# A fixed instruction order for the head of a decoder layer, layer norms on GpSimd, and two transposes moved to DMA

## The chip, the cores and the metric

The kernel runs on one core of one Trainium2 chip. The metric is the device time of one execution in microseconds (us), as the median of several runs. A hardware profiler gives a trace of one further execution; its span runs from the first to the last instruction. The engines are TensorE (PE, with its weight loads apart), VectorE (DVE), ScalarE (ACT), GpSimd (POOL) and SyncE (SP), which here only issues DMAs.

## What is computed

One decoder layer with pre-norms, on x of 8 sequences, 128 tokens, width 512, in float32. `ctx` has the same shape.

```python
x = x + attention(layernorm(x), w_q, w_k, w_v, w_o)   # 32 heads, 8 kv heads, head 128, causal
x = x + cross(ctx, ctx, layernorm(x))                 # softmax(ctx . q^T / sqrt(128)), one head
x = x + ffn(layernorm(x))                             # 4-bit weights, groups of 128 rows
# ffn: (silu(x Wg) * (x Wu)) Wd, inner width 1376
# W[k, n] = q[k, n] * s[g, n] - (z[g, n] + 1) * s[g, n],  g = k // 128
```

The layer norms have no weights; eps is 1e-5. The attention's weights are float32 and random; w_q is 512 x 4096, w_k and w_v 512 x 1024, w_o 4096 x 512.

## The kernel before, in words

**Number format.** PE works in float16 pairs. A tile is split into a high half (cast, on ACT) and a low half (value minus high half, on VectorE or GpSimd): `split` (L115). A product takes three matmuls, high x high, high x low, low x high: `mm3` (L131, L136 to L138). Weights are first brought to a common size: `sumsq` (ACT, L234) sums squares, `scales` casts the sums (L253), adds them over partitions by a matmul with ones (L257, L260) and makes a power-of-two-like factor from them on VectorE (L265, L273, L279). `convert` then scales and splits a weight, in one of two ways: `direct` on ACT and VectorE (L305, L306), or on GpSimd with a cast on ACT (L311, L116, L119).

**Work.** There are 8 kv groups g of 4 heads, and two halves of 4 sequences. A unit is one g and one half; a step is one sequence b of a unit, 64 steps in all. For a unit: `proj_k` (k for all 4 sequences, 12 matmuls of 512 columns), four `proj_q`, and every second group `proj_v` for a pair of groups. For a step: `att_s` (scores into `ps_sc`, masked minimum on VectorE L475, exps on ACT L433, a scaling of the reciprocal `rec` on GpSimd L443, multiplication on GpSimd L489, split into `pb`, and a DMA transpose of `pb` to `pt`, L503), `att_v` (probabilities times v, `ps_at`, L512, L513), and `att_o` (output projection into `ps_o`, added to the residual `xr` on VectorE, L529). v is copied by two DMAs into a second tile `vd` (L420) for the first 64 rows.

**Order.** The program goes through a scheduler that places every instruction by a simulated timeline, by its place in the source and its dependencies. `issue_after` (L122) adds an ordering edge without a wait where the source wants one. Each engine runs its own list in order; SP's list holds all DMAs, and a DMA that waits holds those behind it.

**Head.** The source of the head (after `load_x`, L654) loads x and weights in the order x0, wk, x1, wq in two pieces, x2, x3, wv, x4 to x7, wo, wq and wk of group 1. `load_h` computes a layer norm: statistics on VectorE (L144, L145, L147), the power -0.5 on GpSimd (L151), the application on VectorE (L152), four PE transposes (L347), and a split out of PSUM into the tiles `hTh` and `hTl` of that half. k and q of the first head are projected in three pieces, the first as soon as sequence 0 is there. Twelve warm-up matmuls on zeros (L696) stand in the source after that; the scheduler put them ahead of the first projection. Then come the other q, v, the scores of step 0, the sums of wo, the layer norms of sequences 4 to 7 and the four pieces of wo.

**Scales of the feed-forward weights.** In steps 3 to 5 `col_scales` (L548) loads rows of scales in pieces of 512 columns (L558), casts them to float32 (VectorE, L560), transposes them on PE by pieces of 128 columns (L563) into `ps_st`, copies them out (ACT, L567, L570), and derives ratios from them on VectorE (L573 to L581). In steps 3 to 6 `zeros` unpacks the zero points (VectorE, L602).

Of the kernel before, what the change touches and what calls it, by code (L numbers as in the profile page):

```python
# [18 lines left out]
P = 128  # L19
HQ = 64  # L20
B = 8
# [33 lines left out]
def tile_decoder(  # L55
# [75 lines left out]

    def mm3(ps, parts, start=True, stop=True):

        n = len(parts)
        for i, (lh, ll, rh, rl) in enumerate(parts):
            nc.tensor.matmul(ps, lh, rh, start=start and i == 0, stop=False)  # L136
            nc.tensor.matmul(ps, lh, rl, start=False, stop=False)  # L137
            nc.tensor.matmul(ps, ll, rh, start=False, stop=stop and i == n - 1)  # L138
# [22 lines left out]
    def bank(tag, shape, name):  # L161
# [15 lines left out]
    hT = [  # L177
        [hp.tile([P, KT, TH], F16, name=f"hT{p}{h}", tag=f"hT{p}{h}") for h in range(2)]
        for p in "hl"
    ]  # L180
# [63 lines left out]
    def scales(kind, g, cols=None):  # L244

# [12 lines left out]
        else:  # L258
            for i in range(m):
                nc.tensor.matmul(  # L260
                    ps[:, :1], ones, sb[:, i : i + 1], start=i == 0, stop=i == m - 1
                )
        norm = ONORM if kind == "o" else WNORM
# [15 lines left out]
        nc.vector.reciprocal(sc[:, c0:c1] if kind == "q" else sc, r)  # L279

    def soft_scale(g):
        t = small.tile([P, GH], F32, name="soft", tag="soft")
        nc.vector.tensor_scalar(
            t, sc_t["q", g], sc_t["k", g], -(ASCALE**2) / SCALE, ALU.mult, ALU.mult
        )
        nc.vector.reciprocal(t, t)
        two = small.tile([P, GH // 2], F32, name="soft2", tag="soft2")
        for i in range(2):
            rows = slice(i * HQ, (i + 1) * HQ)
            nc.vector.tensor_copy(  # L290
                two[rows], t[rows].rearrange("p (a i) -> p a i", i=2)[:, :, i]
            )
        soft_t[g] = two
# [38 lines left out]
    def prep_wv(pr, i):  # L332
# [3 lines left out]
        convert(hi, lo, raw_t["v", pr][:, 2 * i : 2 * i + 2, :], sc_t["v", pr])  # L336

    def prep_wo(g, j):
# [3 lines left out]
        convert(hi, lo, raw_t["o", g][:, j, :], sc_t["o", g])  # L342
# [7 lines left out]
    def load_h(b, tag="s"):  # L350
        half, bb = divmod(b, HB)
        h1 = work.tile([P, H], F32, name="h1", tag=tag, bufs=3 if tag == "s" else 1)
        ln = layernorm(h1, xr[b], ASCALE)
        ps = transpose4(h1, "o")
        cs = slice(bb * P, (bb + 1) * P)
        return ln + split(hT[0][half][:, :, cs], hT[1][half][:, :, cs], ps)
# [11 lines left out]
    def proj_q(g, half, j, pieces=(slice(0, TH),)):  # L368
# [7 lines left out]
        for cs in pieces:  # L376
            proj(ps[:, cs], wq_t[g * GH + j], half, cs)
            bs = slice(cs.start // P, cs.stop // P)
# [7 lines left out]
    def proj_k(g, half, pieces=((0, HB),)):  # L386
# [3 lines left out]
        for b0, b1 in pieces:  # L390
            cs = slice(b0 * P, b1 * P)
            proj(ps[:, b0:b1, :].rearrange("p b t -> p (b t)"), wk_t[g], half, cs)
            split(k2[:, b0:b1, 0, :], k2[:, b0:b1, 1, :], ps[:, b0:b1, :])
            yield

    def proj_v(pr, b):
# [14 lines left out]
        mm3(ps, parts)  # L411
        v = vp.tile([P, 2, 2 * P], F16, name="v", tag="v")
# [8 lines left out]
        v_t[pr, b] = v, vd  # L421

# [124 lines left out]

    def col_scales(m, after):  # L548
# [4 lines left out]
        nc.gpsimd.memset(sT[m], 1.0)  # L553
        ps = bank("j", [P, nt, ngr], "ps_st")
        for c0 in range(0, n, H):
            cw = min(n - c0, H)
            s16 = deqp.tile([P, 2 * H], F16, name="s16", tag="qr", bufs=2)
            nc.sync.dma_start(s16[:ngr, :cw], src[:, c0 : c0 + cw])  # L558
            s32 = deqp.tile([P, H], F32, name="s32", tag="qr", bufs=2)
            issue_after(nc.vector.tensor_copy(s32[:ngr, :cw], s16[:ngr, :cw]), after)  # L560
            for k in range(0, cw, P):
                w = min(P, cw - k)
                nc.tensor.transpose(  # L563
                    ps[:w, (c0 + k) // P, :], s32[:ngr, k : k + w], ident[:ngr, :ngr]
                )
        full = n // P
        nc.scalar.copy(sT[m][:, :full, :], ps[:, :full, :])  # L567
        if full < nt:
            w = n - full * P
            nc.scalar.copy(sT[m][:w, full, :], ps[:w, full, :])  # L570
# [16 lines left out]
    NZ = 2 * KT + NFT  # L587
    zt = {}
# [67 lines left out]
    load_x(0)  # L656
    fetch_wk(0)
    load_x(1)
    fetch_wq(0, ((0, 1), (1, GH)))
    load_x(2)  # L660
    load_x(3)
    fetch_wv(0)
    for b in range(HB, B):
        load_x(b)
    fetch_wo(0)
    fetch_wq(1)
    fetch_wk(1)
    halves = (slice(0, P), slice(P, 2 * P), slice(2 * P, 4 * P))
    kgen = proj_k(0, 0, ((0, 1), (1, 2), (2, 4)))
    qgen = proj_q(0, 0, 0, halves)  # L670
    ln0 = load_h(0, "s")
    sumsq("k", 0, 0, 0)
    scales("k", 0)
    ln1 = load_h(1, "s")
    sumsq("q", 0, 0, 0)
    scales("q", 0, (0, 1))
    prep_wk(0, True)
    next(kgen)
    ln2 = load_h(2, "s")
    ln3 = load_h(3, "h1")  # L680
    issue_after(ln1[0], ln0[2])
    issue_after(ln2[0], ln1[2])
    issue_after(ln2[2], ln1[4])
    issue_after(ln3[2], ln1[4])
    prep_wq(0, 0, True)
    next(qgen)
    next(kgen)
    next(qgen)
    next(kgen)
    next(qgen)  # L690

    warm = const.tile([P, TH], BF16, name="warm")
    nc.vector.memset(warm, 0.0)
    ps = bank("a", [P, TH], "ps_w")
    for _ in range(12):
        nc.tensor.matmul(ps, warm[:, :P], warm, start=True, stop=True)  # L696
# [420 lines left out]
```

## Time and profile before

| | |
|---|---|
| Runs | 697.48, 699.82, 700.36 us; median 699.82 |
| Profiled execution | 697.42 us, span 695.6 us |
| PE busy | 654.2 us (94%) |
| DVE busy | 493.3 us (71%) |
| ACT busy | 452.0 us (65%) |
| POOL busy | 375.6 us (54%) |
| Mean granted PE clock | 0.987 |

"Busy" is the time in which an engine runs an instruction. A row of a timeline gives start, length, engine, line of the kernel, operation, output and input by the program's names, their shapes, and in brackets how long the engine was idle before and what ended that. Two matmul rows overlap, since the matmuls are pipelined: the distance of their starts is what one costs. Where the profile speaks of L136 to L138 these are the three matmuls of `mm3`, whoever calls it.

### The profile page before, as it was taken

The numbers are of one execution on the slowest core, as the hardware profiler recorded it, in microseconds if no ns is written. First come the engines' busy times: TensorE is split into PE (matmuls) and PEld (weight loads), VectorE is DVE, ScalarE is ACT, GpSimd is POOL, SyncE is SP. The second block draws the span as 40 slices with busy tenths as digits, with TensorE's granted clock in tenths as the row PEclk, the third lists the DMA queues.
The fourth block names the chain that finished last, engine by engine and source line by source line (L and its number), as shares of the span: only waits on it lengthen the run. The fifth ranks groups of instructions, "written<-read, shape, count | busy, mean of one in ns | idle before, by whom it ended". The sixth has DMA issues, their size and how long they took to land.

```text
span 695.6 us, 12510 instructions
## 1 busy us (share of the span) xinstructions
PE 654.2 (94%) x4099; PEld 376.2 (54%) x4099; DVE 493.3 (71%) x1437; ACT 452.0 (65%) x1274; POOL 375.6 (54%) x573
## 2 busy tenths in 40 slices
PE   5689979999999999999999999999988799999995
PEld 3365544555555545555555555565555445565474
DVE  6774486766757786575778766666678789888986
ACT  4784373766567676655769665454575489968884
POOL 2885184955566896556589696645434723310110
PEclk9999989999999999999999999999999999999998
DMA  9555014455344476244444523422211100002002
GB/s 305 196 133 125 16 37 149 117 147 82 118 104 127 139 154 164 66 122 103 128 141 99 133 65 73 99 57 62 51 42 39 42 1 1 0 1 60 1 1 61
DMA packets 88367, 61.92 MB, mean 89 GB/s; under 512 B 54255, under 2 KB 71706, under 8 KB 88301
## 3 DMA queue, kind: packets, MB, share of 16 engines
q1 hardware_dynamic: 88300, 61.12, 34.1%
q8 instruction: 32, 0.52, 0.3%
q14 instruction: 35, 0.28, 0.1%
HBM read 42.12 MB, written 2.20 MB: 64 GB/s over the span
## 4 chain that ended last, share of the span: by engine, by line
PE 75%; ACT 7%; DVE 6%; POOL 5%; issue 4%; DMA 3%; SPq 0%; DVEq 0%; POOLq 0%; ACTq 0%
PE ps_q L136 7%; PE ps_q L137 7%; PE ps_q L138 7%; PE ps_c L941 7%; PE ps_o L136 7%; PE ps_o L138 7%; PE ps_o L137 7%; PE ps_c L942 6%; PE ps_v L138 2%; PE ps_v L137 2%; PE ps_v L136 2%; PE ps_k L136 2%; PE ps_k L137 2%; PE ps_k L138 2%; DMA pt<-pb 1%
## 5 line engine op out<-in xcount | busy, mean ns | idle before, releaser
L433 ACT ACTIVATE s<-s,negm 128x64 f32<-128x64 f32 (+1 forms) x256 | 93.3, 366 | 56.8 <-DVE negm L475 56.4
L136 PE MATMUL ps_q<-hTh,wqh 128*128 128x512 f16 (+2 forms) x264 | 99.5, 378 | 4.5 <-DVE rs L147 2.4
L137 PE MATMUL ps_q<-hTl,wqh 128*128 128x512 f16 (+2 forms) x264 | 99.3, 377 | 0.0
L138 PE MATMUL ps_q<-hTh,wql 128*128 128x512 f16 (+2 forms) x264 | 99.0, 376 | 0.0
L136 PE MATMUL ps_o<-woh,ah 128*128 128x512 f16 x256 | 98.1, 383 | 0.9 <-ACT ah L116 0.9
L137 PE MATMUL ps_o<-wol,ah 128*128 128x512 f16 x256 | 97.8, 382 | 0.0
L138 PE MATMUL ps_o<-woh,al 128*128 128x512 f16 x256 | 97.6, 381 | 0.0
L529 DVE SCALAR_TENSOR_TENSOR xr<-ps_o,unsc,xr 128x512 f32<-128x512 f32 x64 | 47.9, 749 | 56.6 <-PE ps_o L138 53.7
L443 POOL TENSOR_SCALAR rec<-rec 128x4 f32<-128x4 f32 x64 | 14.1, 221 | 125.7 <-DVE rec L441 125.2
L119 POOL TENSOR_TENSOR pb<-s,pb 128x128 f16<-128x128 f32 (+1 forms) x128 | 72.2, 578 | 7.8 <-ACT pb L116 6.0
L475 DVE CUSTOM_DVE_ANT_0 s<-ps_sc,mask,soft 128x64 f32<-128x64 f32 (+1 forms) x256 | 67.1, 311 | 9.7 <-PE ps_sc L138 7.5
L941 PE MATMUL ps_c<-h3h,nf 128*128 128x512 f16 (+1 forms) x176 | 65.9, 380 | 1.9 <-DVE ps_c L952 1.1
L489 POOL TENSOR_TENSOR s<-s,rec 128x128 f32<-128x128 f32 (+1 forms) x128 | 63.5, 517 | 4.7
L942 PE MATMUL ps_c<-h3l,nf 128*128 128x512 f16 (+1 forms) x176 | 65.7, 379 | 0.0
L119 DVE TENSOR_TENSOR ql<-ps_q,qh 128x512 f16<-128x512 f32 (+2 forms) x66 | 44.2, 669 | 29.4 <-ACT qh L116 29.1
L119 POOL TENSOR_TENSOR il<-pr,ih 128x512 fp32r<-128x512 f32 (+1 forms) x16 | 20.8, 1301 | 77.0 <-ACT ih L116 77.0
L116 ACT CAST ah<-ps_at 128x512 f16<-128x512 f32 x64 | 37.3, 583 | 34.4 <-PE ps_at L138 22.1
L116 ACT CAST pb<-s 128x128 f16<-128x128 f32 (+1 forms) x128 | 43.0, 350 | 25.3 <-POOL s L489 23.9
L116 ACT CAST qh<-ps_q 128x512 f16<-128x512 f32 (+2 forms) x66 | 37.2, 563 | 28.3 <-PE ps_q L138 26.4
L952 DVE TENSOR_SCALAR ps_c<-ps_c,rTg 128x512 f32<-128x512 f32 (+1 forms) x64 | 46.0, 751 | 5.8 <-PE ps_c L942 5.6
L119 DVE TENSOR_TENSOR al<-ps_at,ah 128x512 f16<-128x512 f32 x64 | 43.8, 685 | 6.3 <-ACT ah L116 6.1
L433 ACT ACTIVATION_READ_ACCUMULATOR s<-s,negm 128x1 f32 x256 | 48.1, 188 | 0.0
(196 smaller groups left out, 1766.6 us busy)
## 6 DMA issues: line engine op xcount, KB each, us to landing
rawo<-in_L_attn_w_o_dram SPq DMA_DIRECT2D x8, 1024.0 KB
rawq<-in_L_attn_w_q_dram SPq DMA_DIRECT2D x7, 1024.0 KB, 5.5
zi<-zd SPq DMA_DIRECT2D x26, 256.0 KB, 3.4
vd<-v SPq DMA_DIRECT2D x64, 64.0 KB, 2.1
qr<-_L_ffn_down_qweight_dram SPq DMA_DIRECT2D x10, 256.0 KB, 3.3
xr<-in_x_dram SPq DMA_DIRECT2D x8, 256.0 KB, 7.2
rawk<-in_L_attn_w_k_dram SPq DMA_DIRECT2D x8, 256.0 KB, 3.1
rawv<-in_L_attn_w_v_dram SPq DMA_DIRECT2D x4, 512.0 KB
```

What stands on the lines that cost most here:

```text
L116: a = nc.scalar.copy(hi, src)
L119: b = (lo_eng or nc.vector).tensor_tensor(lo, src, hi, ALU.subtract)
L136: nc.tensor.matmul(ps, lh, rh, start=start and i == 0, stop=False)
L137: nc.tensor.matmul(ps, lh, rl, start=False, stop=False)
L138: nc.tensor.matmul(ps, ll, rh, start=False, stop=stop and i == n - 1)
L433: exp = nc.scalar.activation(v, v, AF.Exp, bias=negm[:, j : j + 1], scale=-1.0, accum_out=sums[:, j : j + 1],)
L475: nc.vector.tensor_tensor_reduce(view, flat(ps, cols[j]), masks[j // 2], soft_t[g][:, j % 2 : j % 2 + 1], BIG, ALU.add, ALU.min, negm,)
L489: mul = nc.gpsimd.tensor_tensor(v, v, rec[:, 2 * k : 2 * k + 2].unsqueeze(2).to_broadcast([P, 2, (k + 1) * HQ]), ALU.mult,)
L529: return nc.vector.scalar_tensor_tensor(xr[b], ps, unsc_t[g], xr[b], ALU.mult, ALU.add)
L941: nc.tensor.matmul(ps, lh, rh, start=r == 0, stop=False, skip_group_check=r > 0)
L942: nc.tensor.matmul(ps, lh, rl, start=False, stop=True, skip_group_check=r > 0)
L952: nc.vector.tensor_scalar(ps, ps, sc, None, ALU.mult)
```

## The change

- **A fixed order.** `in_order` ties every instruction recorded within it to the one recorded before it on the same engine. The whole head, up to the first four v and the first two pieces of wo, moves into a function `begin` that is recorded within it. Generators (`yield` after the matmuls and after the evacuation) let the source interleave the steps by hand. After `begin` the scheduler decides as before.
- **Front.** Ten warm-up matmuls come first. The loads go x0, wk, x1, x2, x3, wq in one piece, wv, x4 to x7, the rest as before. k is projected in two pieces of two sequences, q whole.
- **Layer norms of the head on GpSimd.** VectorE makes the statistics and minus the mean; GpSimd the power and the application (L397 of the new kernel). Sequences 0 to 3 are transposed on PE as before. Sequences 4 to 7 are cast on ACT, their low half is made on GpSimd, and one DMA transpose for each brings both halves to `hT2`, which is now one tile for each half of the sequences. The tile that later takes the layer norm for the feed-forward is joined likewise.
- **Weights.** wv and the first two pieces of wo are converted in the `direct` way.
- **Scales.** All feed-forward scales are loaded into one float16 tile of 32 rows and transposed by one DMA; `col_scales` copies its columns out of that on VectorE.
- **soft_scale** computes two 64-row pieces directly instead of a product and two copies.

```diff
+    @contextmanager
+    def in_order():
+        traced = nc.cur_bb.bb.instructions
+        known = {id(i) for i in traced}
+        yield
+        last = {}
+        for i in nc.cur_bb.bb.instructions:
+            if id(i) in known:
+                continue
+            prev = last.get(i.engine)
+            if prev is not None:
+                tc.add_manual_dep(
+                    i,
+                    prev.name,
+                    mybir.DependencyInfo(
+                        mybir.DependencyClass.NoSync, mybir.DependencyReason.DATA
+                    ),
+                    reason="in_order",
+                )
+            last[i.engine] = i
...
-    hT = [
-        [hp.tile([P, KT, TH], F16, name=f"hT{p}{h}", tag=f"hT{p}{h}") for h in range(2)]
-        for p in "hl"
-    ]
+    hT2 = [hp.tile([P, 2, KT, TH], F16, name=f"hT{h}", tag=f"hT{h}") for h in range(2)]
+    hT = [[t[:, p, :, :] for t in hT2] for p in range(2)]
...
+    def ln_stats(b):
...
+        nc.vector.bn_stats(st, xr[b])
+        nc.vector.bn_aggr(mv, st)
+        rs = small.tile([P, 2], F32, name="rs2", tag="rs2")
+        nc.vector.tensor_scalar(
+            rs[:, 0:1], mv[:, 1:2], EPS, ASCALE**-2, ALU.add, ALU.mult
+        )
+        nc.vector.tensor_scalar(rs[:, 1:2], mv[:, 0:1], -1.0, None, ALU.mult)
+        ln_t["rs", b] = rs
+
+    def ln_apply(b):
+        rs = ln_t.pop(("rs", b))
+        rstd = small.tile([P, 1], F32, name="rstd", tag="rstd")
+        nc.gpsimd.tensor_tensor(rstd, rs[:, 0:1], mhalf, ALU.pow)
+        h = deqp.tile([P, H], F32, name="h", tag=("qr", "zi")[b % 2], bufs=2)
+        nc.gpsimd.tensor_scalar(h, xr[b], rs[:, 1:2], rstd, ALU.add, ALU.mult)
+        ln_t["h", b] = h
...
+    def h_dma(b):
...
+        hb = work.tile([P, 2, H], F16, name="hb", tag="hb")
+        split(hb[:, 0, :], hb[:, 1, :], ln_t.pop(("h", b)), nc.gpsimd)
+        nc.sync.dma_start_transpose(
+            hT2[half].rearrange("p a k t -> p (a k) t")[:, :, cs],
+            hb.rearrange("p a t -> p (a t)"),
+        )
...
+    def scales_load():
+        rows = deqp.tile([SROWS, NFT * P], F16, name="srow", tag="srow")
+        nc.gpsimd.memset(rows, 0.0)
+        for m in "gud":
+            _, _, src, ngr, n = quant[m]
+            nc.sync.dma_start(rows[zrow[m] : zrow[m] + ngr, :n], src)
+        zt["s"] = deqp.tile([P, NFT, SROWS], F16, name="scol", tag="scol")
+        nc.sync.dma_start_transpose(zt["s"], rows)
...
-        for c0 in range(0, n, H):
...
+        ins = nc.vector.tensor_copy(sT[m], zt["s"][:, :nt, zrow[m] : zrow[m] + ngr])
+        issue_after(ins, after)
...
+        kgen = proj_k(0, 0, ((0, 2), (2, 4)))
+        h = {b: h_pe(b) for b in range(HB)}
+        ln_stats(0)
+        sumsq("k", 0, 0, 0)
+        ln_apply(0)
+        sk = scales_parts("k", 0)
+        next(sk)
+        ln_stats(1)
+        next(sk)
+        ln_apply(1)
+        next(h[0])
+        ln_stats(2)
+        ln_apply(2)
+        next(h[0])
+        prep_wk(0, True)
+        next(h[1])
+        ln_stats(3)
+        ln_apply(3)
+        next(h[1])
+        next(h[2])
+        sumsq("q", 0, 0, 0)
+        next(h[3])
+        next(kgen)
...
+        next(q[0])
+        next(q[1])
+        prep_wq(0, 2, True)
+        h_dma(4)
+        ln_stats(6)
+        ln_apply(6)
+        prep_wq(0, 3, True)
+        h_dma(5)
+        next(q[1])
+        next(q[2])
+        prep_wv(0, 0, True)
+        ln_stats(7)
+        ln_apply(7)
+        h_dma(6)
+        prep_wv(0, 1, True)
+        soft_scale(0)
+        h_dma(7)
+        next(q[2])
+        next(q[3])
+        for i in range(2):
+            sumsq("o", 0, i, 0, 2)
+        next(so)
+        next(q[3])
+        v = [proj_v(0, b) for b in range(HB)]
+        next(v[0])
+        next(v[1])
+        next(so)
+        out_scale(0)
+        next(v[0])
+        att_s(0, 0)
+        next(v[2])
...
+    with in_order():
+        begin()
```

## The prediction

> **What bounds the kernel now.** First the page's second part, the busy tenths in 40 slices of 17.4 us. TensorE (PE) is short of full in slices 0 to 2, 5 and 29 to 31 and in the last; in between it is the bound. The change works on slices 0 to 2 and 5.
>
> ```profile
> PE   5689979999999999999999999999988799999995
> ```
>
> Next the table by stage (PE, weight load, DVE, ACT and POOL busy, granted PE clock, DMA share, GB/s).
>
> ```profile
> 12.90:50.00 37.10, 27.63 (x251) 19.74 (x250) 30.61 (x109) 28.75 (x85) 28.12 (x35) 1.00 0.60 193
> 50.00:84.00 34.00, 33.40 (x204) 18.60 (x203) 13.84 (x37) 13.89 (x39) 11.73 (x18) 1.00 0.36 81
> 84.00:94.00 10.00, 7.88 (x74) 4.99 (x73) 8.32 (x38) 8.46 (x37) 7.21 (x13) 0.99 0.11 22
> 94.00:104.00 10.00, 8.49 (x40) 3.89 (x40) 8.40 (x19) 6.12 (x20) 9.80 (x15) 0.84 0.21 42
> 104.00:110.00 6.00, 6.00 (x24) 2.57 (x25) 5.97 (x13) 2.29 (x6) 5.38 (x6) 0.72 0.47 131
> 110.00:510.00 400.00, 399.03 (x2675) 224.69 (x2674) 265.83 (x882) 251.34 (x817) 257.14 (x392) 1.00 0.43 107
> ```
>
> From 110 to 510 us PE idles 1 us of 400, so whatever the change wins or loses by 110 arrives at the end unshortened. Up to 12.9 us no projection runs; from there to 50 PE idles 9.5 us, from 50 to 84 0.6. From 84 to 104 it idles 2.1 + 1.5 = 3.6 us, and in 94 to 110 its clock falls. PE's timeline there shows what for: a scale transpose that waited for VectorE, then projections at half pace.
>
> ```profile
> 93.41 0.38 PE L563 MATMUL ps_st<-ident,s 4*128 4x4 f32 x4 [0.87 <-DVE rec L441]
> 94.05 0.58 PE L136 MATMUL ps_q<-hTh,wqh 128*128 128x512 f16 x1 [0.26 <-DVE r L273]
> ...
> 95.28 0.63 PE L136 MATMUL ps_q<-hTh,wqh 128*128 128x512 f16 x1
> 95.70 0.63 PE L137 MATMUL ps_q<-hTl,wqh 128*128 128x512 f16 x1
> ...
> 97.54 0.38 PE L136 MATMUL ps_q<-hTh,wqh 128*128 128x512 f16 x1
> 97.75 0.38 PE L137 MATMUL ps_q<-hTl,wqh 128*128 128x512 f16 x1
> ```
>
> Start to start is 0.43 us until 97, 0.215 after; 104 to 107.5 repeats it. The transposes cost a share of PE, the wait, and the clock.
>
> **What the Trainium skill says.** "TensorE: Matmul & The Clock Gate", Part 1: the array falls to half rate after an idle window of about 3.4 us and needs a busy one to come back. The 0.43 against 0.215 agrees. Part 4 there says transposes don't count as work for this gate; no row shows that alone. "SBUF — State Buffer", section "SBUF: two separate sides": VectorE and GpSimd hold a common port pair exclusively, for a whole instruction. The trace agrees: two 64x2 copies took 2.04 us while GpSimd multiplied weights.
>
> ```profile
> 22.47 1.19 DVE L306 SCALAR_TENSOR_TENSOR wql<-rawq,scq,wqh 128x512 f16<-128x512 f32 x1
> 24.65 2.04 DVE L290 COPY soft<-soft 64x2 f32<-64x2 f32 x2
> ```
>
> "GPSIMD Engine Reference", 4.1: one-input operations run near line rate, two-input ones about twice as long. A 128x512 cast took 0.61 us, the two-input subtraction 1.16.
>
> **Part 1, the head.** Scores of step 0 end on PE at 37.7 us now; its probabilities are finished on GpSimd (pb) at 48.87, and PE takes them up (ps_at) at 52.73 after their DMA transpose. I follow the changed order, read from the built program, engine by engine with the durations above (back-to-back starts lie about 0.09 us closer than durations).
> - Warm-up: ten matmuls of 0.43 from 1.35 to 5.6 us, where PE has nothing else. It was twelve, 8.78 to 13.06, just ahead of the first projection. Now only layer norm transposes follow for 7 us, so I expect the clock down again at the first projection: k (24 matmuls of 256 columns) takes 5.1 instead of 2.6 us until it comes back, say +2.
> - Layer norms 0 to 3: pow 0.55 + apply on GpSimd. No row shows the apply; 0.61 (the cast) is the lower bound, 1.04 (two-input multiply) the upper; I take 0.65. Norm 3 follows wk's low half on VectorE (ends 9.75), its statistics end at 10.7, h3 at 12.0, its transposes at 12.7. In the fixed order these stand ahead of k: it starts at 12.7 (now 12.89, one block). Nothing is gained there, though x arrives sooner (wq, 1 MB, lands about 11 us by bytes delivered, and only delays sums of squares).
> - k ends at 17.4, q0 runs 17.5 to 20.1, q1 waits for the scales of v (ACT's 1.1 us sum at 20, then VectorE) and runs 21.3 to 23.9, q2 and q3 wait little and end at 29.6. Now q3 ends at 35.4.
> - Then a new wait. ACT copies the last layer norm (hb of 7) ahead of q2's evacuation and wo's two sums (2.35). h7 waits for VectorE (statistics of 7 stand behind wv's low half) and for GpSimd: pow, apply, and the low half of 5 (1.16) ahead of it. With collisions on the port pair I get h7 at 31.45, hb 32.0, q2 32.6, sums 34.9. Two scale matmuls for wo, which stand ahead of v on PE, need them: PE idles 29.6 to 35.2 and its clock may fall. Then v0, v1 (2.6, +0.8 for the clock), scores 0: 39 us.
> - ACT then holds q3, four sums of wq (2.9), v0, k's sum (0.7) ahead of the first exps, so rec reaches GpSimd at 41.5 (now 40.65). From there to pb GpSimd's rows are the same 7.1 us: rec, two multiplies 0.97, wq 1.04, again, wk 1.04, pb 1.06. It now waits 1.65 among them (rec at 44.58), then less. pb is ready at 48.6, taken up at 52.5. PE has only k left to do before that (until 48), and idles 4.5.
> - What is behind: pb of step 1 comes 2.1 us after pb of 0 now; in the new order rec, wq, pb, multiplies, wq, pb (.22 + 1.16 + .43 + .97 + 1.05 + .69) make it 4.5. On SP's queue six copies of v (0.55 each) now also stand between the two transposes (1.23 + 3.3 = 4.5). Step 1 is taken up at 57.1 and ends at 57.65, with the same matmuls done as at 54.53 now. PE is full from there; the next equal point (end of step 2's ps_at) is 68.4 now, then 57.65 + 13.5 of matmuls = 71.1. **Head: +2.7**, from -0.5 (warm clock, no collisions, h7 2.5 sooner) to +6 (apply at 1.04, every low half hit).
> - Four norms leave PE (16 transposes, 2.1 us in two bursts at 40 and 44), ACT/VectorE evacuations become copies of like length, and four DMA transposes go on SP (1.23 us to issue by pt's row; 4/3 of its data, landing about 4 by its 3.0). The last lands near 38, k's half 1 needs it at 45: hidden by 7 us; without cover about 4. Weight loads queued behind these transposes (wq 2, wv 1) have over 20 us. wo's first two matrices go to ACT/VectorE (0.72, 0.74) instead of GpSimd (2.2), not early enough to shorten the chain.
>
> **Part 2, the scales.** Gone: 26 transposes on PE, seven groups together 2.7 us; seven casts on VectorE (0.3 to 1.3, 5.8 in all), four of them over 0.9, by my reading with the port pair taken; five ACT copies; seven small loads on SP's queue, the last issued at 99.72, ahead of the transpose (100.15) that PE waited 1.24 us for at 102.9. New: three loads and one DMA transpose on SP in the head, a memset, three 128x44 copies on VectorE (bounds 0.15 and 1.1; I take 0.5 each), all beside slack. The stage from 84 to 110 holds 3.6 idle + 3.3 clock + 2.7 transposes = 9.6 us. Not all comes back: ACT's late q cast (0.61) and the r wait (0.26) stay, and GpSimd is the next limit. From rec of step 4 (2.3 us after its scores) to pb of step 7 it has 4 x 2.25 + 4.1 + 3.5 + 2.1 + 1.2 = 19.9 us, + 3.9 for the transpose: 26.1. PE needs about 27.4 for the same stretch. PE leads by so little that I leave 2.1 of stalls: **-7.5**, between -4 and -9.5.
>
> **Part 3, the rest.** soft_scale trades two copies (0.62 on average) and a tensor_scalar (0.46) for two tensor_scalars per group, beside PE's matmuls on an engine 66% busy from 110 to 510: 0; on the path it would be -0.8 for one group in the head. h3's two tiles become one: reads of the same times release it: 0. The middle of the program keeps its order on PE; from the last attention steps on it is shuffled in places: 0, +-1.5.
>
> Sum +2.7 - 7.5 + 0 = -4.8, against the profiled execution's 697.42 (span 695.6): 692.6. The runs' median, 699.82, lies 2.4 above that; taken from it, **695.0**.
>
> **Rivals.** (a) GpSimd takes the place of the transposes: the stage gives 4 only. For: POOL busy 9.80 of 94 to 104. Against: nothing on GpSimd is held by it at 110. 2.7 - 4 = -1.3: 698.5. (b) The head costs nothing or wins: warm clock, few collisions, h7 by 29. For: ACT is idle 2.9 us in one place before 14 us. -0.5 to -1 - 7.5: 691.5. (c) Slower: the copy of h7 on ACT. With apply at 1.04 and each low half meeting VectorE it comes at 36 or later; everything behind it, q2's evacuation to the exps, moves as much, PE idles over 8 us, the clock is low for v and k: head +7.5. With the stage at -4: 703.3. It decides from a head of +7.5 on if the stage gives 7.5, from +4 on if it gives 4. (d) The order isn't held, or the later one shuffled so that the stage keeps other stalls: the built order excludes the first; the second is in (a).
>
> **Numbers.** Forecast 0.43, (a) 0.25, (b) 0.20, (c) 0.12. Half a per cent, 3.5 us, is about what this measurement can tell from no change. Faster: 0.36 of the forecast, all of (b), a little of (a), 0.58; slower: most of (c) and the far end of (a), 0.12; same 0.30. 690 to 702 holds (b)'s lower end down to -10, (a) and the near part of (c). The forecast alone: 692.5 to 697.5.
>
> **What would show it.** No ps_st and PE at 0.215 us a matmul between 84 and 110; a PE gap of about 5 us near 30 ahead of ps_n; hb of 7 on ACT right ahead of q2; ps_at of step 0 near 52.5 and of step 1 near 57; k at 0.21 us per 256 columns at 13 us. Wrong if ps_at of step 0 comes by 49, or later than 55, or if half-rate stretches stay near 95.

## The result, and the profile after

The changed kernel takes 704.11 us (median of 7 runs, 702.08 to 704.79), the kernel before in the same session 699.82 (7 runs). The ratio is 1.0074, with a 95% interval of 1.0048 to 1.0100: slower by 3.4 to 7 us. The profiled execution took 702.08 us with a span of 700.2 us; before it was 697.42 and 695.6.

The busy tenths of TensorE in 40 slices (now 17.5 us each):

```profile
PE   6757999799999999999999999999988889899995
```

Slices 1 to 3 were 6, 8, 9 and are now 7, 5, 7: the loss is in the head. Slice 5, which was 7, is now 9; in its place slice 7 fell from 9 to 7. The same stages as in the prediction (PE, weight load, DVE, ACT and POOL busy, granted PE clock, DMA share, GB/s):

```profile
12.90:50.00 37.10, 25.61 (x153) 15.31 (x152) 20.10 (x70) 19.43 (x46) 13.68 (x14) 0.76 0.69 196
50.00:84.00 34.00, 28.66 (x181) 16.98 (x179) 16.24 (x51) 21.20 (x62) 22.38 (x32) 0.95 0.42 115
84.00:94.00 10.00, 10.00 (x59) 4.79 (x58) 4.78 (x25) 2.31 (x9) 0.00 (x0) 1.00 0.09 20
94.00:104.00 10.00, 10.00 (x76) 5.58 (x75) 6.70 (x27) 8.20 (x32) 8.62 (x14) 1.00 0.15 30
104.00:110.00 6.00, 6.00 (x37) 3.01 (x35) 4.64 (x21) 6.00 (x22) 5.41 (x11) 1.00 0.11 22
110.00:510.00 400.00, 396.30 (x2644) 222.37 (x2643) 266.83 (x873) 250.12 (x810) 264.48 (x400) 1.00 0.44 108
```

From 12.9 to 50 us TensorE does 153 instructions where it did 251, at a clock of 0.76 (before 1.00). ScalarE, too, is busy 19.4 us there instead of 28.8, GpSimd 13.7 instead of 28.1. The engines that were to be relieved are not overloaded, they wait. From 84 to 110 TensorE is full and at full clock, as forecast. From 110 on it idles 3.7 us where it idled 1.

Where the lateness comes and goes is read from the end of each step's `ps_at` against the kernel before: step 0 +7.2 us, step 1 +11.1, step 2 +11.0, step 4 +11.5, step 7 +1.6, step 12 +4.4, step 40 +3.3, step 63 +1.4, end of the span +4.6. So the head costs 11 in this pair of traces, the stage of the scales wins 9.4, steps 8 to 12 give back 2.8, and after step 63 another 3.2 are lost (1.9 of them had been won between steps 40 and 63). By the columns of the matmul rows both kernels have done the same work at steps 2, 12, 40 and 63, but at step 7 the changed one is further by what I estimate at 0.8 us of matmuls. In equal work the stage wins about 10.2 and steps 8 to 12 give back 3.6, the length of the stall shown below.

**The head.** TensorE's longest wait, and the instruction that starts after it:

```profile
41.72 0.19 PE L284 MATMUL ps_n<-sb,ones 128*128 128x1 bf16 x2 [9.05 <-DVE sb L277]
```

`sb` holds the sums of wo. Those are made by ScalarE, whose timeline ahead of them reads:

```profile
31.65 0.62 ACT L116 CAST hb<-h 128x512 f16<-128x512 f32 x1 [2.97 <-DMA hT<-hb]
...
38.13 0.62 ACT L116 CAST hb<-h 128x512 f16<-128x512 f32 x1 [5.24 <-DMA hT<-hb]
38.66 0.58 ACT L116 CAST qh<-ps_q 128x512 f16<-128x512 f32 x1
39.13 1.06 ACT L254 ACTIVATE junk<-rawo 128x1024 bf16<-128x1024 f32 x1
```

Layer norm 7 was there at 33.59, by GpSimd's row:

```profile
32.82 0.77 POOL L397 TENSOR_SCALAR h<-xr,rs,rstd 128x512 f32<-128x512 f32 x1
```

Its cast to `hb` began at 38.13, released by a DMA: `hb` is a tile of a pool with two buffers, so norm 7 needs the buffer of norm 5, which its DMA transpose was still reading. Behind the cast, in the fixed order, stand the evacuation of q2 and both sums of wo. And that transpose was slow, as SP's queue shows:

```profile
30.26 0.54 SPq L216 DMA_DIRECT2D rawq<-in_L_attn_w_q_dram  x1
30.90 0.69 SPq L683 DMA_DIRECT2D qr<-_L_ffn_gate_qweight_dram  x1
32.23 1.39 SPq L414 DMA_TRANSPOSE hT<-hb  x1
```

It was issued at 32.23, 2 us after a load of 1 MB and 1.3 us after one of 256 KB, and released its buffer at 38.1: 5.9 us. The first one (issued at 28.51, before these loads) took 3.1.

**Steps 8 to 12.** The stall that gives back part of the scales' gain, on SP and on TensorE:

```profile
118.03 0.27 SPq L675 DMA_DIRECT2D zd<-z  x1
...
126.27 0.82 SPq L691 DMA_DIRECT2D zi<-zd  x2
127.20 2.70 SPq L568 DMA_TRANSPOSE pt<-pb  x2
```

```profile
131.37 0.28 PE L577 MATMUL ps_at<-pt,vd 128*128 128x256 f16 x1 [3.59 <-DMA pt<-pb]
```

The zero-point loads `zi` read what the store `zd` wrote. They could start 8.2 us after it was issued, and the attention transposes stand behind them on SP, although GpSimd had finished the `pb` of step 8 at 122.8. Before, the first of these loads went at 119.72 and the transpose behind it at 120.63; TensorE took its result up at 125.97 without a wait:

```profile
114.11 0.27 SPq L615 DMA_DIRECT2D zd<-z  x1
119.72 0.81 SPq L631 DMA_DIRECT2D zi<-zd  x2
120.63 1.23 SPq L503 DMA_TRANSPOSE pt<-pb  x1
```

### The profile page after: what moved, and what is told of

The parts are those of the page before. It is cut to its first block, busy times and chain, and to the rows that moved or that the text cites. A ratio compares the mean times of both kernels' runs of the same rounds, so it can differ in the third digit from the quotient of the medians.

```text
span 700.2 us, 12337 instructions
## 1 busy us (share of the span) xinstructions
PE 653.5 (93%) x4019; PEld 372.1 (53%) x4019; DVE 484.5 (69%) x1424; ACT 454.5 (65%) x1268; POOL 376.4 (54%) x571
## 4 chain that ended last, share of the span: by engine, by line
PE 72%; ACT 9%; DVE 6%; issue 5%; POOL 4%; DMA 3%; SPq 0%; DVEq 0%; POOLq 0%; ACTq 0%
PE ps_o L158 7%; PE ps_o L160 7%; PE ps_o L159 7%; PE ps_q L160 7%; PE ps_q L158 7%; PE ps_q L159 7%; PE ps_c L1048 6%; PE ps_c L1049 6%; PE ps_v L160 2%; PE ps_v L158 2%; PE ps_v L159 2%; PE ps_k L158 2%; PE ps_k L160 2%; PE ps_k L159 2%; DMA pt<-pb 1%
## 5 line engine op out<-in xcount | busy, mean ns | idle before, releaser
L158 PE MATMUL ps_q<-hT,wqh 128*128 128x512 f16 x256 | 97.3, 380 | 0.4 <-DVE ql L119 0.3
L160 PE MATMUL ps_q<-hT,wql 128*128 128x512 f16 x256 | 97.0, 379 | 0.3 <-DVE wql L333 0.3
L159 PE MATMUL ps_q<-hT,wqh 128*128 128x512 f16 x256 | 97.1, 379 | 0.0
L119 POOL TENSOR_TENSOR pb<-s,pb 128x256 f16<-128x256 f32 (+1 forms) x128 | 72.6, 580 | 9.8 <-ACT pb L116 8.0
L540 DVE CUSTOM_DVE_ANT_0 s<-ps_sc,mask,soft 128x64 f32<-128x64 f32 (+1 forms) x256 | 67.4, 312 | 10.4 <-PE ps_sc L160 6.4
L119 DVE TENSOR_TENSOR ql<-ps_q,qh 128x512 f16<-128x512 f32 x64 | 44.0, 688 | 40.9 <-ACT qh L116 40.7
L1048 PE MATMUL ps_c<-h,nf 128*128 128x512 f16 (+1 forms) x176 | 66.1, 380 | 3.9 <-ACT sg L1075 1.5
L1049 PE MATMUL ps_c<-h,nf 128*128 128x512 f16 (+1 forms) x176 | 65.9, 379 | 0.0
L116 ACT CAST pb<-s 128x256 f16<-128x256 f32 (+1 forms) x128 | 42.7, 349 | 27.8 <-POOL s L554 27.5
L116 ACT CAST ah<-ps_at 128x512 f16<-128x512 f32 x64 | 37.3, 583 | 34.1 <-PE ps_at L160 20.7
L116 ACT CAST qh<-ps_q 128x512 f16<-128x512 f32 x64 | 36.9, 576 | 19.9 <-PE ps_q L160 19.7
```

The costliest lines, as they stand in the source:

```text
L116: a = nc.scalar.copy(hi, src)
L119: b = (lo_eng or nc.vector).tensor_tensor(lo, src, hi, ALU.subtract)
L540: nc.vector.tensor_tensor_reduce(view, flat(ps, cols[j]), masks[j // 2], soft_t[g][:, j % 2 : j % 2 + 1], BIG, ALU.add, ALU.min, negm,)
L1048: nc.tensor.matmul(ps, lh, rh, start=r == 0, stop=False, skip_group_check=r > 0)
L1049: nc.tensor.matmul(ps, lh, rl, start=False, stop=True, skip_group_check=r > 0)
```

## The experiments

Eighteen kernels ran, in sets that share a chip and the runs of the kernel before. Each time is a median of 5 to 22 runs; the ratio to the kernel before has its 95% interval in brackets. The sets ran on different chips. The kernel before has medians from 698.96 to 699.82 in them, so a difference between two sets can be off by up to 0.9 us for that reason alone. In single traces one and the same head ends up to 6 us apart (last section), so verdicts use medians, and traces are used for places.

**Four buffers for hb.**

```diff
-        hb = work.tile([P, 2, H], F16, name="hb", tag="hb")
+        hb = work.tile([P, 2, H], F16, name="hb", tag="hb", bufs=4)
```

> The changed kernel, with four buffers for hb instead of two. Theory (reuse wait): in the changed kernel ScalarE's cast of layer norm 7 stood ready at 33.6 us and began at 38.1, because its buffer still fed the DMA transpose of norm 5; q2's evacuation and wo's sums stand behind it. With four buffers the cast comes at about 33.7, TensorE's wait ahead of ps_n falls from 9.05 to about 4.6 us, ps_at of step 2 ends about 4.5 us sooner (75 instead of 79.5), and the total is about 699.5 (698 to 701), against 704.1. Rival 1 (the slow layer norms on GpSimd set the time, the buffer wait is hidden behind them): the wait stays over 7.5 us and the total within 1.5 of 704.1. Rival 2 (freed early, lost later): the wait falls, but the scheduler's later order or the stall at step 8 takes it back; total 702 to 704.

697.6 us, 0.9976 [0.9961, 0.9992]. The cast of norm 7 starts at 32.47 and is now released by GpSimd (`h`), not by a DMA; TensorE's wait is 4.74:

```profile
36.05 0.19 PE L284 MATMUL ps_n<-sb,ones 128*128 128x1 bf16 x2 [4.74 <-DVE sb L277]
```

The reuse wait is shown, and worth 6.5 us between the medians, more than the 4.5 us of its own length. Not all of it is the buffer's own. TensorE's wait fell by 4.3 us. Another 2.4 are the stall of step 8, of which 1.23 us are left: the scheduler, which works on a changed program here, put one attention transpose more ahead of the zero-point loads on SP. The clock from 12.9 to 50 us was 0.87 instead of 0.76.

**The bulk loads behind the transposes**, two buffers as they were (the same call stands around the loads of wk, wv and the 4-bit weights):

```diff
+    def late(ins):
+        if "dma" in ln_t:
+            issue_after(ins, ln_t["dma"])
...
-            nc.sync.dma_start(raw[:, :, a * P : b * P], src[:, :, a * P : b * P])
+            late(nc.sync.dma_start(raw[:, :, a * P : b * P], src[:, :, a * P : b * P]))
...
-        nc.sync.dma_start_transpose(
+        ln_t["dma"] = nc.sync.dma_start_transpose(
```

> The changed kernel with two buffers for hb as it is, but the loads of the next wq (1 MB), wv and the first 4-bit weights are ordered on SP behind the last of the four layer norm transposes. Theory (the second transpose landed after 5.9 us instead of 3.1 because it shared the DMA engines with the 1 MB load issued 2 us ahead of it): it lands at about 35.3 instead of 38.1, the cast of norm 7 begins then, TensorE's wait falls by 2.5 to 3 us to about 6.3, total about 701.3. Rival (the transposes run one after the other or are slow in themselves): landing stays over 5 us, total 703.5 to 705.

699.29 us, 1.0008 [0.9982, 1.0033]. TensorE waits 6.29 us. The cast comes at 35.97 and all transposes now land after 3.0 us:

```profile
35.97 0.62 ACT L116 CAST hb<-h 128x512 f16<-128x512 f32 x1 [2.48 <-DMA hT<-hb]
```

So the second transpose was slow because of the loads ahead of it; which of the two, the run doesn't tell. 2 us more were won than expected. The trace shows a place for them: the stall at step 8 is 1.08 us instead of 3.59. As with four buffers, the scheduler put an attention transpose (117.67 us) between the store `zd` and the loads `zi`, where the changed kernel has none:

```profile
128.73 0.28 PE L583 MATMUL ps_at<-pt,vd 128*128 128x256 f16 x1 [1.08 <-DMA pt<-pb]
```

**One part alone.** First the scales on the old head (`scales_load` and the new `col_scales` put into the kernel before), then the new head with the old scales:

> The kernel before with only the scales of the feed-forward weights changed to the one DMA transpose; its head is the old one. Theory: the stage from 84 to 110 us runs without idle time and at full clock as in the changed kernel; -9.4 us there, less what a stall at step 8 (attention transpose behind zero-point loads on SP) may give back (about 3): total 690 to 693.5 against 699.8 for the kernel before. Rival (the gain seen in the changed kernel was only slack that its late head had left, or it needs the new order): the stage gives 4 or less, total 696 or more.

697.89 us, 0.9977 [0.9957, 0.9997]: only 1.7 us faster between the medians, against my expectation. In its trace the stage has no idle time at full clock, and step 7 ends 8.6 us ahead of the kernel before; but step 12 ends only 3.9 ahead, and the tail after step 63 takes 154.3 us instead of 151.6. The gain is real and given back twice. The first place is step 8, where TensorE waits; from 110 to 150 us its clock is 0.96. The first `pb` halves for this step were there at 113.3, but their transposes stand behind the loads `zi` on SP and went at 118.08:

```profile
117.15 0.82 SPq L626 DMA_DIRECT2D zi<-zd  x2
118.08 2.69 SPq L503 DMA_TRANSPOSE pt<-pb  x2
122.46 0.40 PE L512 MATMUL ps_at<-pt,vd 128*128 128x256 f16 x1 [3.73 <-DVE negm L475]
```

> The changed kernel with the old way of the scales (26 transposes on TensorE); so only the new head. Theory: ps_at of step 2 about 11 us later than in the kernel before (79.5 against 68.4), and the loss reaches the end: total 708 to 712. Rival (a late head is partly caught up in the stage from 84 to 110, where TensorE had idled): total 702 to 706, and then the scales are worth less on top of the new head than the sum of parts says.

705.25 us, 1.0089 [1.0064, 1.0113]. The rival's range. Step 2 ends 10.4 us late in this trace, but its profiled execution lay 3.4 us above its median, and that of the kernel before 2.4 below. The new head costs about 6 us in the medians. +5.6 and -1.7 make +3.9; the whole change has +4.3: the parts add.

**The zero-point loads behind the attention transpose**, once with the new head and four buffers, once with the old head:

```diff
-        nc.sync.dma_start(
+        ins = nc.sync.dma_start(
             zi[:p, :n],
             zt["d"][row : row + 1, c0:c1].to_broadcast([p, n]),
         )
+        if m == "g" and g == 0:
+            issue_after(ins, st_p["dma"])
```

Here `st_p["dma"]` is the last attention transpose recorded.

> The changed kernel with four buffers for hb, and the first three zero-point loads (zi) ordered on SP behind the attention transpose of the following step. Theory (in the changed kernel the zero-point loads, which waited 8 us for the store zd to land, stood on SP ahead of attention transposes whose probabilities were ready 4 us earlier): TensorE's wait of ps_at on pt at steps 7 to 9 vanishes (1.23 us here with four buffers, 3.59 in the changed kernel), and the total falls by 1.5 to 2.5 us against four buffers alone (697.6), to about 695.6. Rival (the transpose is late for another reason, GpSimd's pb or VectorE): PE still waits over 1 us between 110 and 130 and the total stays within 1 of 697.6.

695.87 us, 0.9955 [0.994, 0.997]: 1.7 below four buffers alone. TensorE is full from 100 to 140 us.

> The kernel before with its old head, the scales by one DMA transpose, and the same order of the zero-point loads. With the scales alone the gain was 8.6 us at the end of step 7 and 3.9 at the end of step 12. Theory (4 to 5 us of it were lost to the zero-point loads on SP): at step 12 about 8 ahead of the kernel before, total about 694 against 697.9 with the scales alone. Rival (the stall there, 3.7 us of idle TensorE ahead of ps_at, has another cause, VectorE's negm as the profile names it): total within 1 of 697.9.

695.97 us, 0.9959 [0.994, 0.9977]: 1.9 below the scales alone in medians, between theory and rival. The sizes agree with each other; the intervals of each pair overlap, and against the kernel before of its own set each gain is only 1.1 to 1.3 us, so the amount is uncertain. The 8 us at step 12 did not come: it ends 2.3 ahead, in a trace whose head was 4.6 us later at step 2. The place is shown, though. With the transposes ahead of the loads on SP (117.19 and 122.25 us) the wait of 3.73, which the profile had put down to VectorE, is 0.66:

```profile
123.22 0.28 PE L512 MATMUL ps_at<-pt,vd 128*128 128x256 f16 x1 [0.66 <-DMA pt<-pb]
```

The next version with the old head, under the tail below, has the same edges; its trace's head was not late, and step 12 ends 7.0 ahead.

**The tail in its old order.** The edits change how the scheduler orders the end of the program: from the first load of the cross-attention on, 608 of TensorE's 930 instructions stand in another place than before. They are the same instructions. So the old order can be imposed, by edges without waits between neighbours, on TensorE, VectorE, ScalarE and GpSimd (`TAIL` has no list for SP):

```diff
+    def pin(known):
...
+            for a, b in zip(order, order[1:]):
+                tc.add_manual_dep(
+                    seq[b],
+                    seq[a].name,
...
+    pin(tail)
```

> The changed kernel with four buffers for hb, and from the first load of the cross-attention (step 57) on every engine's instructions in the order that the scheduler chose in the kernel before. Theory (the scheduler ordered the tail anew, 608 of TensorE's 930 instructions there stand elsewhere, and that order is slower): the time from the end of step 63's ps_at to the end falls from 155.0 us to about 151.6, total about 694.4 against 697.6 with four buffers alone. Rival (the tail is slower because of the data or of what precedes it, not of its order): 154 to 155, total within 1 of 697.6.

693.55 us, 0.9915 [0.9891, 0.994], 4 us below four buffers alone; after step 63 it takes 151.3 us instead of 155.0. Shown, for this version.

> All three: the changed kernel with four buffers for hb, the zero-point loads behind the attention transposes, and the tail in the order of the kernel before. If the three losses are separate places they add: 697.6 - 2 - 3.2 = 692.4 (691 to 694), faster than both kernels. Rival (an earlier arrival at one place only moves the wait to the next): 694.5 or more.

690.97 us, 0.9892 [0.9867, 0.9916]. They add, and this is 8.0 us faster than the kernel before in the same set (698.96).

> The changed kernel with nothing but its tail (from step 57's first cross-attention load) in the order of the kernel before. Theory (the tail's loss stands by itself): 704.1 - 4.3 = 699.8 (698.5 to 701), the time from the end of step 63 to the end falls from 154.8 to 151.4. Rival (it is coupled to what arrives before it): 702 or more.

701.92 us, 1.0043 [1.0022, 1.0064], between theory and rival. Only 2.2 of the expected 4.3, and the intervals overlap. In the medians the order of the tail is worth 2 to 5 us. In the traces the stretch after step 63 is steady: 150.9 to 152.3 us in the nine with the old order, 152.8 to 156.6 in all others. Steps 57 to 63 are not: in the nine they take 48.9 to 51.3 us. In this pair the 2.7 us that are won after step 63 are lost there (51.3 instead of 48.7), and why is not shown.

> The old head: the kernel before with the scales by one DMA transpose, the zero-point loads behind the attention transposes, and the tail in the order of the kernel before. It has everything of the last version but the new head. Theory (with four buffers the new head is worth nothing, since its gains in TensorE's work are paid in idle time and half clock): within 1.5 of the 690.97 of the version with the new head, about 692. Rival 1 (the new head still costs 2 to 4 us, as the ends of steps 1 to 4 suggest): 687 to 689. Rival 2 (the new head gains, which single traces of the head, which differ by up to 4 us with one and the same program, would hide): 694 or more.

692.66 us, 0.9916 [0.9892, 0.994]: 1.7 above 690.97, just outside the theory's 1.5 and short of rival 2. The intervals overlap, and against the kernel before of its own set (699.66) the difference is 1.0. With its buffers mended, the fixed head of the change is worth nothing against the old head that these runs can tell from zero. The 3.3 us against the old head without the tail's order are not placed by the traces: 1.4 are won after step 63 (152.3 against 153.7), but steps 57 to 63 take 50.9 us instead of 48.9.

**Inside the fixed head.** Three edits of the version of 690.97. Warm-ups in TensorE's gaps (`warms(3)` after three transposes, `warms(16)` after q3):

> The version of 690.97 us with 25 more warm-up matmuls: three after each of the first three layer norm transposes, 16 in the idle stretch after q3. Theory (the clock had fallen at the first k piece and again at v after the idle stretch): k's matmuls of 256 columns take 0.11 instead of 0.21 us from the start, v's too, together 2.5 to 4 us on TensorE; as the first scores come 2 to 3 us sooner the total falls by 2 to 3, to about 688.5. Rival (the end of the head is set by GpSimd's and VectorE's rows between the scores and pb, not by TensorE): the matmuls are faster and the total stays within 1 of 690.97.

690.22 us, 0.9872 [0.9835, 0.9908]: within 1, the rival. The matmuls are faster (k's first 12 in 1.47 us, in the unaltered version 2.77), and TensorE waits longer instead, 3.0 us for v where it had waited 2.2, and 2.3 for the `pt` of step 1. The cold clock was there; what it cost at the end, 0.75 us between the medians (1.4 against the kernel before of its own set), is not clear of noise.

All eight norms transposed on TensorE:

> The version of 690.97 us with all eight layer norms transposed on TensorE: sequences 4 to 7 in the idle stretch after q3, evacuated by ScalarE and VectorE, no DMA transposes and no low halves on GpSimd. Theory (the four DMA transposes themselves cost nothing once their buffers suffice; TensorE's 16 transposes fall into idle time): within 1 of 690.97. Rival (GpSimd's four low halves, 1.2 to 1.6 us each, had delayed layer norm 7 and so wo's sums): norm 7 comes 3 us sooner, total about 688.5.

695.6 us, 0.9951 [0.9935, 0.9968]: 4.6 slower, against both. TensorE still waits 3.11 us for wo's sums, then another transpose and v follow at half clock. In this fixed order the DMA is the better way for four of the norms.

The sums of wo moved behind q3's evacuation, their two matmuls behind v and scores:

> The version of 690.97 us (fixed order, four buffers, zero-point loads and tail ordered) with the sums of wo behind q3's evacuation on ScalarE and their two matmuls behind the first scores and v of sequence 2 on TensorE, still in a fixed order. Theory (the two matmuls ahead of v hold TensorE 4.74 us): the wait falls to 1.5 to 2.5 us (v then waits for wv's second low half, about 34), the first scores come 2 to 3 us sooner, total 688 to 689.5. Rival (the free order wins by its earlier layer norms and sums, and the first scores' successors on GpSimd and VectorE set the end of the head): within 1 of 690.97.

691.43 us, 0.9903 [0.9869, 0.9936]: the rival. The wait of 4.74 is gone, TensorE waits 3.04 for q2's low half instead, and step 1 ends 3.8 us later. Moving this one group of instructions was not enough.

**Without the fixed order.** First on the version of 690.97 (`begin()` called outside `in_order()`):

> The version of 690.97 us (new head, four buffers, zero-point loads and tail ordered), but the new head is recorded without the fixed order, so that the scheduler places its instructions. Theory (the fixed order of the head is not what costs; its own waits are for ScalarE's sums of wo and GpSimd): within 2 of 690.97. Rival (the hand-made order is worth several us, or costs them): below 688 or above 694.

686.34 us, 0.9813 [0.9776, 0.9849]: 4.6 faster, with the tail in the same order in both. My expectation fell, so the order of the head became the suspect. The changed kernel with this one edit and nothing mended:

```diff
-    with in_order():
-        begin()
+    begin()
```

> The changed kernel with the fixed order of the head taken away and nothing else: two buffers for hb, zero-point loads and tail as the scheduler places them. Theory (the fixed order is what costs: it puts the last layer norm and wo's sums at 33 to 41 us on ScalarE though ScalarE and GpSimd stood idle before 23 us): total 5 to 9 below 704.1, 695 to 699, the rest above 686.3 being the tail (4.3) and the zero-point loads. Rival (the two buffers cost as much in any order): within 3 of 704.1.

683.78 us, 0.9776 [0.9752, 0.9799]. It is the fastest of all and far below the 695 to 699 that I expected: 20 us below the changed kernel and 16 below the kernel before, with two buffers, and without the edges for loads or tail. On the free order these remedies bring nothing: with all of them it had 686.34. Between the two traces (680.3 against 700.2) 15.7 us are won by the end of step 12, 3.2 in steps 57 to 63 and 1.9 after them. The stages of its head:

```profile
12.90:50.00 37.10, 29.67 (x205) 18.26 (x204) 27.32 (x105) 30.74 (x86) 24.80 (x31) 0.92 0.87 235
50.00:84.00 34.00, 33.30 (x209) 18.96 (x209) 15.19 (x52) 16.12 (x51) 14.79 (x25) 1.00 0.34 83
```

ScalarE does 30.7 us of work by 50 us instead of 19.4. Its timeline shows which:

```profile
18.00 1.06 ACT L254 ACTIVATE junk<-rawo 128x1024 bf16<-128x1024 f32 x1
...
20.70 1.05 ACT L254 ACTIVATE junk<-rawo 128x1024 bf16<-128x1024 f32 x1
...
35.56 0.62 ACT L116 CAST hb<-h 128x512 f16<-128x512 f32 x1 [2.81 <-DMA hT<-hb]
36.09 0.58 ACT L116 CAST qh<-ps_q 128x512 f16<-128x512 f32 x1
```

The sums of wo run at 18 and 20.7, where ScalarE had time and the data had come, instead of 39.1 and 40.3. The cast of the last norm still waits 2.81 us for its buffer, but only the evacuation of one q stands behind it.

Last, the order was freed on ScalarE alone, kept on TensorE alone, and free with four buffers:

```diff
-            if id(i) in known:
+            if id(i) in known or i.engine == mybir.EngineType.Activation:
```

> The changed kernel with the fixed order on every engine but ScalarE. Theory (ScalarE's order is what stops TensorE: behind the cast of norm 7 stand q2's evacuation and wo's sums): TensorE's wait of 9.05 us ahead of ps_n falls below 3 us though hb has two buffers, and total 690 to 696, most of the way from 704.1 to 683.8. Rival 1 (TensorE's and VectorE's orders cost as much): 698 or more. Rival 2 (ScalarE alone is all of it): 686 or less.

693.98 us, 0.9933 [0.9907, 0.9958]. TensorE's wait, two buffers as they were:

```profile
PE ps_n L284 <- DVE sb L277: 1.5, 1, 1.5
```

It was 9.05. One of ScalarE's casts still waits 2.04 us for a buffer and starts at 40.1, even later than before; two evacuations of v and the first exps stand behind it, but no longer q2's evacuation and wo's sums. Step 12 ends 9.7 us sooner than in the changed kernel.

> The changed kernel with the fixed order on TensorE alone; the scheduler places all other engines' instructions. Theory (the other engines' orders cost, TensorE's own little): 684 to 690. Rival (v standing behind wo's two sum matmuls, and k whole ahead of q, are the price): 695 or more.

687.63 us, 0.9844 [0.9818, 0.987]: as expected. Its trace tells where the 3.9 us above the free order lie: step 12 ends at 142.5 us, 1.9 ahead of the free one, but steps 57 to 63 take 50.9 us instead of 45.5. In these two traces TensorE's fixed order in the head costs nothing; the difference is in the end of the program.

> The changed kernel without the fixed order and with four buffers for hb. Theory (in the free order the cast of norm 7 still waits 2.81 us for a buffer, but only the evacuation of the last q stands behind it): within 1.5 of 683.78. Rival (that wait is on the way to the first scores): 681 or less.

684.62 us, 0.9797 [0.9771, 0.9824]: as expected; the buffers that were worth 6.5 us in the fixed order are worth nothing in the free one.

## Why the prediction was wrong, point by point

The forecast was 695.0, the result 704.1. Two terms of the sum failed. In the medians of the parts the head came as +5.6 instead of +2.7, mainly because of a buffer that the working had left out, and the scales as -1.7 instead of -7.5, because most of what they win in their stage is lost after it. With the buffer mended the total is 697.6, inside the stated range, but that would have been luck in part: the head then costs about nothing (697.6 against 697.9 with the old head), and the scales still bring far less than forecast.

- **Warm-up, k and q.** Right within about 3 us. k started at 13.24 (forecast 12.7) at half clock, and q3 ended at 32.7 (29.6): the second k piece waited 1 us for the evacuation of the first, and q0 began at half clock too. That the cold clock adds 2 us at the end is not borne out: with it warm, 0.75 us were won, within the noise.
- **The new wait ahead of ps_n, the first step that failed.** The place was right: norm 7's cast on ScalarE, q2's evacuation and wo's sums behind it, TensorE idle. The working timed the cast by norm 7 alone (31.45) and didn't ask whose buffer it writes. Norm 7 came at 33.59, the cast at 38.13, and TensorE idled 9.05 us instead of 5.6; with the buffer mended 4.74. The forecast did say that these transposes land about 4 us after issue and are "hidden by 7 us", counting k's half 1 as their only reader. The buffer was a second party waiting for the landing.
- **From the scores to step 1.** Right: 5.0 us between the two ends of `ps_at` (forecast 4.5), with v's copies between the two transposes on SP, all of it some 8 us later.
- **Head +2.7.** Measured +11.0 in the traces, about +6 in the medians (705.25 alone, and 704.1 against 697.9 beside the new scales).
- **Scales -7.5, the second step that failed, and the larger part of the miss.** The mechanism and the stage were right: no idle time, full clock, -9.4 from step 2 to step 7. The sum failed in what follows. "Whatever the change wins or loses by 110 arrives at the end unshortened" did not hold: with the old head 8.6 us at step 7 became 3.9 at step 12 and 1.7 in the medians. The zero-point loads on SP, which held the attention transpose, are the first place; the tail is the second. Edges for them bring 1.9 and 3.3 of that back in the medians. (The half rate near 95 us agrees with what the prediction cites only in the two rates. The idle window of its source does not stand ahead of it in the trace: from 90.04 to 94.05 us TensorE was busy 1.88 us, transposes included.)
- **The rest 0 ± 1.5.** Missed in place, hidden in the sum: +3.2 after step 63, but -2.9 between steps 12 and 63. The tail's order is worth 2 to 5 us in the medians of the experiments.
- **Rival (c)** named the side, the place and nearly the time (703.3), but by another mechanism: slow norms and collisions. Norm 7 would have had to come at 36; it came at 33.6. So it is not confirmed; that its time is near the result is luck.

What none of the cases held is that the fixed order itself is the largest term: 704.1 with it, 694.0 with ScalarE freed, 687.6 with all but TensorE freed, 683.8 without. Part of these differences is the tail's order, which changes with each. By the end of step 12, where all have done the same matmuls, the single traces stand at 160.0, 150.3, 142.5 and 144.4 us. Why the free order is better in the head is shown for ScalarE by its timeline; for VectorE, GpSimd and SP only by the total. Why the scheduler's order of steps 57 to 63 is faster after a free head stays open.

## What to carry to other kernels

Ahead of a step that writes a rotating buffer, ask who read that buffer last and when that reader's DMA lands, and then list what stands behind the writer on its engine: that decides what the wait costs, and not its length (TensorE's wait fell by 4.3 us with the buffer mended; where the order was free, nothing was won). An order written by hand turns each late item into a stop for its engine, so compare it first with the same source left to the scheduler. Then take away remedies that were made for the fixed order: here they brought nothing once it was gone. And a gain in one stage counts only after the next in-order queue has been checked for what now arrives too early: here loads that wait for a store, ahead of the transposes that TensorE needs.

## What the runs showed of the hardware that I had not expected

- A DMA transpose of 256 KB took 3.0 to 3.1 us to land with no load issued just ahead of it, and 5.9 when loads of 1 MB and 256 KB had been issued 2.0 and 1.3 us before.
- The clock of TensorE in one and the same head differs from run to run. The old head ended step 0 at 52.93, 53.44 and 54.26 us in three traces (clock 1.00 throughout) and at 59.01 in a fourth (0.92 from 20 to 30 us, 0.91 from 30 to 40, 0.83 from 50 to 60). TensorE's instructions up to there stand in the same order in all four. What made the clock fall in the fourth is not shown.
- Layer norm transposes with gaps don't keep the clock up. The changed kernel, with only those between 5.6 and 13.2 us, and the version with nine warm-ups among them:

```profile
13.00:16.00 3.00, 3.00 (x16) 2.09 (x15) 0.71 (x2) 0.59 (x1) 0.00 (x0) 0.50 1.05 388
```

```profile
0.00:12.90 12.90, 8.76 (x32) 3.91 (x32) 7.75 (x28) 5.77 (x11) 9.19 (x23) 1.00 0.87 278
12.90:50.00 37.10, 29.28 (x204) 17.67 (x206) 25.05 (x103) 28.88 (x79) 21.73 (x29) 0.95 0.70 205
```

  This agrees with the Trainium skill, "TensorE: Matmul & The Clock Gate", Part 1, that the array is at half rate after an idle window, and Part 4, that transposes don't count as work for this; no run here separates the gaps from the transposes.
- GpSimd's layer norm application (one input, two scalars, 128x512) took 0.77 us, and 1.31 where it started together with a weight conversion on VectorE (29.78 us); the power of 128 values took 0.55, and 1.05 where such a conversion had started just before (28.62). Where GpSimd's application had started first (26.16), it kept its 0.77 and VectorE's conversion took 1.02 instead of 0.74.
